# One token list per expert for both router choices, with the weighted rows added to the output by the scatter itself

## The chip, the cores and the metric

The kernel runs on one core of a Trainium2 chip. The metric is the device time of one execution in microseconds (us); the profile shows one execution of its own, with its span from the first to the last instruction.

## The reference, cut to what matters

The input is 2048 tokens (8 batches of 256) of 512 numbers. A gated cross attention is added to each token, and then a gated mixture of 8 experts, of which each token uses the two with the highest router probability:

```
x = x + tanh(g_xattn) * cross_attention(layernorm(x), ctx, mask)
h = layernorm(x)
p = softmax(h @ w_router.T)                  # 8 experts
v, i = top_k(p, 2);  v = v / sum(v)
x = x + tanh(g_ffn) * sum over the two choices k:
        v[k] * (silu(h @ w_gate[i[k]].T) * (h @ w_up[i[k]].T)) @ w_down[i[k]].T
```

An expert has 192 inner columns. All numbers are 32-bit floats.

## The kernel before

**Attention stage.** The tokens are cut into 16 tiles of 128. The order of the instructions on every engine is written by hand: a loop over steps `s` calls the parts of a tile (`a_scores`, `a_probs`, `a_values`) and of a pair of tiles (`f_scale`, `f_weigh`, `f_mark`, `f_rank`, `f_table`, `f_count`) at fixed offsets, and each engine works through its own list in that order. `a_values` (line 397) adds the attention to the residual tile in `xall`. `f_weigh` finishes a pair's rows `xr`: 512 centred columns, the router logits, the negative mean `NM`, the two choice weights `W1` and `W2` and two scales. It stores them to a table `xc_d` in memory with a DMA issued by ACT (line 427, 576 KB each, eight of them). Loads are issued by SP in the same loop: `load_batch` brings the transposed tokens of a batch, three buffers deep, and `load_half` brings one half of an expert's weights (`wgu` 768 KB or `wd` 384 KB) in each of the steps 2 to 17.

**Routing.** For each choice there is a separate list of tokens per expert, filled up to whole tiles of 128. `f_mark`, `f_rank` and `f_count` count with matmuls into `rank`; `f_table` writes the token numbers into `table` with matmuls. The factors `ac` of these (line 458) are made on POOL. At the end, `numbers`, `read_table` and `experts` turn this into `ids`, the row numbers of every list tile, and `eqi`, the expert of every tile.

**Expert stage.** `run` goes over 19 tiles of the first choice and then 19 tiles of the second. For a tile `q`, POOL issues an indirect gather of 128 rows of `xc_d` into a ring of eight buffers that lies over `xall` (line 681); it is issued four tiles ahead. PE transposes the rows (`turn`, line 183), multiplies by `wgu_sb` (`gate_up`, line 699), transposes the result (`flip`, line 714) and multiplies by `wd_sb` (`down`, line 723). The expert of the tile is a register, so the slices of `wgu_sb` and `wd_sb` are addressed at run time, and the first `gate_up` waits for the loads of all experts' `wgu`. ACT applies the choice's weight while it copies the result to `y` (line 727). A first-choice tile then adds the residual on DVE (line 729) and POOL scatters it to a second table `acc_d` (line 686). A second-choice tile gathers its rows of `acc_d`, adds them on DVE (`add`, line 736, one step after `down`) and POOL scatters the sum to `out`. The scatters are declared independent of each other (`free`), so none waits for the one before it. Unused places of a tile gather one row of zeros, and the scatter drops them. If a list needs more than 19 tiles, a branch (`more_tiles`) runs the rest one after the other; it stands once between the two lists and once at the end.

Of the kernel before, what the change touches and what calls it, by code (L numbers as in the profile page):

```python
# [28 lines left out]
NL = 2 * E  # L29
LT = T // P  # L30
NQ = NT + E - 1
Q2 = NQ
NS = 2 * NQ
CV = 64
NP = B // 2
N0 = NT + 3
E1 = E + 1
LG, NM, W1, W2, RS, R2 = D, D + E, D + E1, D + E1 + 1, D + E1 + 2, D + E1 + 3
XU = D + E1 + 4
# [7 lines left out]
def gated_xattn_moe(ctx: ExitStack, tc: tile.TileContext, x, xT, ctxn, ctxT, mask, maskT, g_x, g_f, wr, wgu, wd, out):  # L47
# [84 lines left out]
    ntg = const.tile([P, 1], FP, name="ntg")  # L132
# [12 lines left out]
    xc_d = dr.tile([T + 1, XW], FP, name="xc_d")  # L145
    acc_d = dr.tile([T + 1, D], FP, name="acc_d")
# [3 lines left out]
    table = bank([P, 2, P], "table")  # L150
# [3 lines left out]
    ecol = const.tile([P, 2, E], FP, name="ecol")  # L154
    lbase = const.tile([1, P], FP, name="lbase")
    ltile = const.tile([P, 2, E], FP, name="ltile")
    keep = const.tile([P, 2, E], FP, name="keep")
    cols = const.tile([P, P], FP, name="cols")
    idt = const.tile([P, NT], FP, name="idt")
# [6 lines left out]
    marks = [rt.tile([P, 2 * NL + P], FP, name=f"mark_{k}") for k in range(2)]  # L166
# [3 lines left out]
    spacer = const.tile([1, 1], FP, name="spacer")  # L170
# [68 lines left out]
    def m_gates():  # L239
        nc.vector.tensor_scalar(few, KEEP["most"], float(CV), None, ALU.is_le)  # L240
        nc.vector.tensor_scalar(vgt, cnt, 1.0, few, ALU.min, ALU.mult)
        nc.vector.tensor_scalar(ntg, tg[:, 1:2], -1.0, None, ALU.mult)
        nc.vector.tensor_scalar(vgt, vgt, tg[:, 0:1], None, ALU.mult)
        pairs = vgt.rearrange("p (n h) -> p h n", h=2)
        for h in range(2):
            nc.vector.tensor_copy(vcol[h * CV:(h + 1) * CV, :], pairs[h * CV:(h + 1) * CV, h, :])
        nc.vector.tensor_scalar(nvcol, vcol, -1.0, None, ALU.mult)
# [171 lines left out]
    def f_weigh(k):  # L419
# [5 lines left out]
        nc.scalar.activation(xr[:, :, W1], d, AF.Identity, bias=tg[:, 1:2], scale=ntg)  # L425
        nc.scalar.activation(xr[:, :, W2], d, AF.Identity, bias=tg[:, 1:2], scale=tg[:, 1:2])
        nc.scalar.dma_start(out=xc_d[2 * k * P:2 * (k + 1) * P, :].rearrange("(t p) c -> p t c", p=P), in_=xr)

    def f_mark(k):
        m = marks[k % 2][:, NL:3 * NL]  # L430
        nc.vector.tensor_tensor(m.rearrange("p (t k e) -> p t k e", t=2, k=2), ecol.unsqueeze(1).broadcast_to([P, 2, 2, E]),
                                ix[:, 2 * k:2 * k + 2, 0:2].unsqueeze(3).broadcast_to([P, 2, 2, E]), ALU.is_equal)

# [3 lines left out]
    def f_rank(k):  # L437
        more(k, below, NL)
        more(k, ones, 0)
        at = sm_.tile([P, 2 * NL], FP, tag="at", bufs=2, name=f"at_{k}")  # L440
        nc.vector.tensor_mul(at, marks[k % 2][:, NL:3 * NL], rank[:, 0:2 * NL])
        pos = sm_.tile([P, 4], I32, tag="pos", bufs=2, name=f"pos_{k}")
        with nc.allow_low_precision(reason="whole numbers under 2 ** 16"):
            nc.vector.tensor_reduce(pos, at.rearrange("p (n e) -> p n e", n=4), AX.X, ALU.add)
# [10 lines left out]
        for n in range(4):  # L455
            i = 2 * k + n // 2
            by = nc.vector if last and n < 2 else nc.gpsimd
            by.tensor_scalar(at_col[:, n, :], cols, low[:, n:n + 1], idt[:, i:i + 1], ALU.is_equal, ALU.mult)  # L458
        KEEP["at", k] = at_row, at_col

    def f_table(k):

        at_row, at_col = KEEP.pop(("at", k))
        for n in range(4):
            nc.tensor.matmul(table[:, n % 2, :], lhsT=at_row[:, n, :], rhs=at_col[:, n, :], start=False, stop=True,  # L465
                             skip_group_check=True)

    def f_count(k):
        more(k, rest, NL)
        more(k, ones, 2 * NL)  # L470

    def free(inst, group):

        nc.gpsimd.memset(spacer, 0.0)
        inst = inst.ins
        tc.declare_no_dep(inst, group=group, reason="other rows")
        tc.add_to_no_dep_group(group, inst)

    def constants():
# [4 lines left out]
        nc.gpsimd.iota(lbase[:, 0:2 * NL].rearrange("o (t k e) -> o t k e", t=2, k=2), pattern=[[0, 2], [0, 2], [T, E]], base=0, channel_multiplier=0,  # L484
# [7 lines left out]
    def more_constants():  # L492
        any_ = dict(allow_small_or_imprecise_dtypes=True)
        nc.gpsimd.iota(ecol, pattern=[[0, 2], [1, E]], base=0, channel_multiplier=0, **any_)
# [5 lines left out]
        nc.gpsimd.iota(idt, pattern=[[P, NT]], base=-T, channel_multiplier=1, **any_)  # L500
        for t in xrs:
            nc.gpsimd.memset(t[:, :, XU:XW], 0.0)
        nc.gpsimd.dma_start(out=xc_d[T:T + 1, :], in_=zero)
        nc.gpsimd.dma_start(out=acc_d[T:T + 1, :], in_=zero[:, 0:D])

    def last_constants():
        any_ = dict(allow_small_or_imprecise_dtypes=True)
        nc.gpsimd.iota(ltile, pattern=[[0, 2], [-LT, E]], base=0, channel_multiplier=0, **any_)
        nc.gpsimd.memset(keep, 1.0)
        nc.gpsimd.memset(keep[:, 1, 0:1], 0.0)  # L510
# [14 lines left out]

    ids = rt.tile([P, NS], U32, name="ids")
    eqi = rt.tile([1, NS], I32, name="eqi")
    nt_i = rt.tile([1, 2], I32, name="nt_i")
    sel = rt.tile([P, 2, NQ], FP, name="sel")

    end = rt.tile([P, 2, E], FP, name="end")

    def numbers():

        u = rt.tile([P, 2, E], I32, name="u")
        uf, lf = u.rearrange("p k e -> p (k e)"), ltile.rearrange("p k e -> p (k e)")
        nc.vector.tensor_scalar(uf, rank[:, 0:NL], float(P - 1), None, ALU.add)
        nc.vector.tensor_scalar(uf, uf, 7, None, ALU.arith_shift_right)
        nti = rt.tile([P, 2, E], FP, name="nti")
        nf = nti.rearrange("p k e -> p (k e)")  # L540
        nc.vector.tensor_tensor(nf, uf, lf, ALU.add)
        nc.vector.tensor_tensor_scan(end.rearrange("p k e -> p (k e)"), keep.rearrange("p k e -> p (k e)"), nf, 0.0,
                                     ALU.mult, ALU.add)
        nc.vector.tensor_sub(nti, end, nti)
        nc.vector.tensor_mul(nti, nti, rowe.unsqueeze(1).broadcast_to([P, 2, E]))
        begin = rt.tile([P, 2], FP, name="begin")
        nc.vector.tensor_reduce(begin, nti, AX.X, ALU.add)
        for k in range(2):
            nc.vector.tensor_scalar(sel[:, k, :], qplace, begin[:, k:k + 1], None, ALU.is_equal)

    def experts():
        past = row([P, NS * E], "past")[0:1].rearrange("o (k q e) -> o k q e", k=2, q=NQ)
        nc.vector.tensor_tensor(past, end[0:1].unsqueeze(2).broadcast_to([1, 2, NQ, E]),
                                cols[0:1, 0:NQ].unsqueeze(1).unsqueeze(3).broadcast_to([1, 2, NQ, E]), ALU.is_le)
        pn = rt.tile([1, NS], FP, name="pn")
        nc.vector.tensor_reduce(pn, past.rearrange("o k q e -> o (k q) e"), AX.X, ALU.add)
        nc.vector.tensor_scalar(eqi, pn, float(E - 1), None, ALU.min)
        nc.vector.tensor_copy(nt_i, end[0:1, :, E - 1])

    def read_table():  # L560
        tb = row([P, 2, P], "tb")
        nc.scalar.copy(tb, table)
        pid = bank([P, NS], "pid")
        for k in range(2):
            nc.tensor.matmul(pid[:, k * NQ:(k + 1) * NQ], lhsT=tb[:, k, :], rhs=sel[:, k, :], start=True, stop=True)
        nc.vector.tensor_scalar(ids, pid, float(T), None, ALU.add)
# [5 lines left out]
    with tc.manual_schedule(engines={PE, DVE, ACT, POOL, SP}):  # L572
# [32 lines left out]
        for s in range(NT + 2):  # L605
# [32 lines left out]
            if s == 1:  # L638
                nc.tensor.matmul(rank, lhsT=ones[0:1, :], rhs=lbase, start=True, stop=True)
                nc.tensor.matmul(table.rearrange("p k r -> p (k r)"), lhsT=ones[0:1, :], rhs=zero[:, 0:2 * P], start=True, stop=True)  # L640
# [22 lines left out]
            if part == 0 and 0 < p < NP:  # L663
                m_route(p)
            if not odd and 3 <= (s + 4) // 2 < B:
                load_batch((s + 4) // 2)
            if 2 <= s < 2 + 2 * E:
                load_half(s - 2)

# [3 lines left out]
    def gather(src, q, name):  # L673
        if name == "xg":
            k = RING if apart else KEEP["ring"]
            g = xall.rearrange("p i d -> p (i d)")[:, k * XW:(k + 1) * XW]
            if not apart:
                KEEP["ring"] = (k + 1) % RING
        else:
            g = row([P, D], f"{name}_{q}")  # L680
        nc.gpsimd.indirect_dma_start(out=g, out_offset=None, in_=src[:, :],  # L681
                                     in_offset=bass.IndirectOffsetOnAxis(ap=ids[:, q:q + 1], axis=0))
        KEEP[name, q] = g

    def scatter(dst, q, z, group):
        free(nc.gpsimd.indirect_dma_start(out=dst, out_offset=bass.IndirectOffsetOnAxis(ap=ids[:, q:q + 1], axis=0),  # L686
                                          in_=z, in_offset=None, bounds_check=T - 1, oob_is_err=False), group)
# [31 lines left out]
    def down(q):  # L719
# [6 lines left out]
        c = W1 if q < Q2 else W2  # L726
        nc.scalar.activation(y, py, AF.Copy, scale=xg[:, c:c + 1])  # L727
        if q < Q2:
            nc.vector.scalar_tensor_tensor(y, xg[:, 0:D], xg[:, NM:NM + 1], y, ALU.subtract, ALU.add)  # L729
            scatter(acc_d[:, :], q, y, "acc")  # L730
        else:
            KEEP["y", q] = y

    def add(q):
        y, a = KEEP.pop(("y", q)), KEEP.pop(("acc", q))
        nc.vector.tensor_add(y, y, a)  # L736
        scatter(out, q, y, "out")

    AHEAD, LAG = 4, 3

    def run(qs, side=None, after=None):

        n = len(qs)

        def at(f, s, *more):
            if 0 <= s < n:
                f(*more[:1], qs[s], *more[1:]) if more else f(qs[s])
        for s in range(min(AHEAD, n)):
            at(gather, s, xc_d, "xg")
        for s in range(min(2, n)):  # L750
            at(turn, s)
        for s in range(n + LAG):
# [67 lines left out]
```

## Time and profile before

| what | value |
|---|---|
| median of 3 runs | 300.09 us (299.21 to 300.32) |
| the profiled execution, its own time | 298.8 us |
| its span | 297.0 us |
| PE busy | 265.2 us, 89% of the span |
| POOL busy | 152.8 us, 51% |
| DVE, ACT busy | 133.2 us (45%), 114.6 us (39%) |
| DMA | 48.55 MB, 163 GB/s over the span |
| granted TensorE clock, mean | 0.96 |

The profiled execution took 1.8 us more than its span, and is 1.3 us under the median. In the page a line such as L699 is a line of the kernel's code; PE is TensorE, PEld its weight loads, POOL is GpSimd, SP the engine that issues most loads. "Landing" of a DMA is the moment at which its semaphore tells that all of it has arrived.

### The profile page before, as it was taken

How to read it: one execution, taken by the hardware profiler on the slowest of the kernel's cores; microseconds unless marked ns; L12 is line 12 of the kernel's file. 1: busy time of each engine (PE TensorE's matmuls, PEld its weight loads, DVE VectorE, ACT ScalarE, POOL GpSimd, SP SyncE). 2: the span in 40 equal slices, each digit the busy share in tenths (PEclk: the TensorE clock that was granted, in tenths of full speed). 3: DMA queues.
4: the chain of work that ended last, by engine and by line, in shares of the span. 5: the costliest groups of instructions: out<-in, count | busy, mean ns of one | idle time of the engine just before them, and what ended most of it. 6: DMA issues, size and time to landing. Idle time of an engine off the chain costs nothing.

```text
span 297.0 us, 4010 instructions
## 1 busy us (share of the span) xinstructions
PE 265.2 (89%) x1106; PEld 167.1 (56%) x1106; DVE 133.2 (45%) x450; ACT 114.6 (39%) x275; POOL 152.8 (51%) x239
## 2 busy tenths in 40 slices
PE   5489688979963899999999999998999999999990
PEld 4186477767742565656565656564555555555550
DVE  3438878887772033333333333333233333252441
ACT  2123567777770133333333333332322432333330
POOL 4508964647574502534343434342677578465452
PEclk9959999999995599999999999999999999999997
DMA  4599847999425702232414232422465456444422
GB/s 144 202 355 384 300 164 236 295 341 360 183 104 177 230 8 74 78 115 93 135 48 138 95 124 92 122 100 78 117 206 191 138 171 210 152 142 121 141 78 98
DMA packets 16077, 48.55 MB, mean 163 GB/s; under 512 B 3181, under 2 KB 3181, under 8 KB 16048
## 3 DMA queue, kind: packets, MB, share of 16 engines
q0 software_dynamic: 7984, 25.64, 27.5%
q1 hardware_dynamic: 5888, 17.85, 17.5%
q10 hardware_dynamic: 2176, 4.72, 4.1%
q8 instruction: 13, 0.21, 0.3%
q14 instruction: 16, 0.13, 0.1%
HBM read 35.08 MB, written 14.68 MB: 168 GB/s over the span
## 4 chain that ended last, share of the span: by engine, by line
PE 45%; POOL 15%; issue 15%; DMA 8%; ACT 6%; DVE 4%; ACTq 0%; POOLq 0%; another core or an unknown queue 0%
PE pgu L699 19%; PE py L723 10%; POOL out L686 5%; POOL acc L681 4%; POOL xall L681 4%; DMA xall<-xc_d,ids 4%; PE pt_g L183 3%; PE psc L361 3%; DMA cn<-ctxn,gid 3%; PE table L465 2%; PE pav L391 2%; PE pht L714 1%; PE pc L279 1%; PE ppt L389 1%; DMA acc<-acc_d,ids 1%
## 5 line engine op out<-in xcount | busy, mean ns | idle before, releaser
L699 PE MATMUL pgu<-wgu_sb,xT_g 128*128 x304 | 106.1, 492 | 0.9 <-ACTq L772 0.9
L699 PEld LDWEIGHTS pgu<-wgu_sb,xT_g 128*128 128x128 f32 x304 | 58.1, 192 | 49.3 <-issue 17.7
L723 PE MATMUL py<-wd_sb,hT 96*128 x152 | 71.4, 592 | 0.0
L705 DVE SCALAR_TENSOR_TENSOR th<-th,pgu 128x192 f32<-128x192 f32 x38 | 13.4, 354 | 96.6 <-ACT th L704 71.6
L686 POOL DMA_INDIRECT acc_d<-y,ids x19 | 19.3, 1018 | 60.4 <-DVE y L729 57.8
L681 POOL DMA_INDIRECT xall<-xc_d,ids x38 | 38.7, 1018 | 13.1 <-issue 6.2
L704 ACT ACTIVATE th<-pgu,xall 128x192 f32<-128x192 f32 x38 | 16.0, 420 | 72.4 <-PE pgu L699 55.9
L727 ACT ACTIVATE y<-py,xall 128x512 f32<-128x512 f32 x38 | 26.1, 688 | 37.7 <-PE py L723 29.3
L723 PEld LDWEIGHTS py<-wd_sb,hT 96*128 96x128 f32 x152 | 25.9, 190 | 18.7 <-issue 18.7
L185 ACT COPY xT_g<-pt_g 128x512 f32<-128x512 f32 x38 | 22.2, 585 | 26.3 <-PE pt_g L183 15.4
L458 POOL TENSOR_SCALAR ac<-cols,low,idt 128x128 f32<-128x128 f32 x30 | 25.4, 856 | 11.6 <-DVE low L448 11.5
L686 POOL DMA_INDIRECT out<-y,ids x19 | 20.0, 1051 | 21.6 <-DVE y L736 16.1
L183 PE MATMUL pt_g<-ident,xall 128*128 128x128 f32 x152 | 23.8, 281 | 5.5 <-issue 4.9
L729 DVE SCALAR_TENSOR_TENSOR y<-xall,y 128x512 f32<-128x512 f32 x19 | 14.3, 751 | 28.7 <-ACT y L727 27.2
L681 POOL DMA_INDIRECT acc<-acc_d,ids x19 | 18.3, 963 | 9.7 <-issue 9.7
L183 PEld LDWEIGHTS pt_g<-ident,xall 128*128 128x128 f32 x152 | 18.3, 144 | 6.6 <-issue 5.5
L361 PE MATMUL psc<-cT,xT 128*128 128x137 f32 x128 | 19.6, 301 | 1.3 <-issue 0.7
L361 PEld LDWEIGHTS psc<-cT,xT 128*128 128x128 f32 x128 | 17.9, 208 | 2.0 <-issue 1.1
L714 PEld LDWEIGHTS pht<-ident,h 128*96 128x96 f32 x76 | 9.6, 126 | 12.7 <-issue 7.6
L391 PE MATMUL pav<-cn,prT 128*128 128x512 f32 x32 | 16.4, 594 | 0.0
L707 DVE SCALAR_TENSOR_TENSOR h<-th,xall,pgu 128x192 f32<-128x192 f32 x38 | 15.7, 414 | 1.4
L716 DVE COPY hT<-pht 96x256 f32<-96x256 f32 x38 | 15.8, 415 | 0.6 <-remote 0.4
(156 smaller groups left out, 298.6 us busy)
## 6 DMA issues: line engine op xcount, KB each, us to landing
wgu_sb<-wgu SPq DMA_DIRECT2D x8, 768.0 KB, 7.2
xc_d<-xr ACTq DMA_DIRECT2D x8, 576.0 KB, 7.7
xT<-xT SPq DMA_DIRECT2D x8, 512.0 KB, 5.8
wd_sb<-wd SPq DMA_DIRECT2D x8, 384.0 KB, 7.1
xall<-x SPq DMA_DIRECT2D x1, 2048.0 KB
xall<-x SPq DMA_DIRECT2D x2, 512.0 KB
xall<-x SPq DMA_DIRECT2D x1, 1024.0 KB, 6.9
xall<-xc_d,ids POOLq DMA_INDIRECT x38
```

The costliest lines, as they stand in the source:

```text
L183: nc.tensor.transpose(pt[:, c, :], src[:, c * P:(c + 1) * P], ident)
L185: nc.scalar.copy(dst, pt)
L361: nc.tensor.matmul(both, lhsT=xTs[b][:, c, t * P:(t + 1) * P], rhs=cTs[p % 2][:, c, :], start=(c == 0), stop=(c == HC - 1))
L391: nc.tensor.matmul(pav, lhsT=prT, rhs=cns[p], start=True, stop=True)
L458: by.tensor_scalar(at_col[:, n, :], cols, low[:, n:n + 1], idt[:, i:i + 1], ALU.is_equal, ALU.mult)
L681: nc.gpsimd.indirect_dma_start(out=g, out_offset=None, in_=src[:, :], in_offset=bass.IndirectOffsetOnAxis(ap=ids[:, q:q + 1], axis=0))
L686: free(nc.gpsimd.indirect_dma_start(out=dst, out_offset=bass.IndirectOffsetOnAxis(ap=ids[:, q:q + 1], axis=0), in_=z, in_offset=None, boun ...
L699: nc.tensor.matmul(pgu, lhsT=xgT[:, c, :], rhs=wgu_sb[:, bass.ds(v * GU + c * 2 * I, 2 * I)], start=(c == 0), stop=(c == HC - 1))
L704: nc.scalar.activation(th, pgu[:, 0:I], AF.Tanh, scale=xg[:, RS:RS + 1])
L716: nc.vector.tensor_copy(hT, pht)
L723: nc.tensor.matmul(py, lhsT=hT[:, k, :], rhs=wd_sb[:, bass.ds(v * DN + k * D, D)], start=(k == 0), stop=(k == 1))
L727: nc.scalar.activation(y, py, AF.Copy, scale=xg[:, c:c + 1])
```

## The change

The two lists are merged into one list per expert, in which a token stands twice, under two experts. The list has 36 tiles (`N0 = 2 * NT + 4`), with up to 39 places in all. Which choice a place belongs to is told by the sign and size of its number in `table` (`idt` has two columns), and `read_table` makes from it `ids` and a `sign` of -1 or +1. Instead of `W1` and `W2` a row holds one number `DW`, and DVE makes each tile's weight column `w` from `DW`, `sign` and the gate.

The residual no longer goes through the expert stage. A new `x_store` writes each pair of finished residual tiles (512 KB) from `xall` to `out` through SP's queue in the attention loop. In the expert stage, every tile's weighted `y` is scattered to `out` by POOL with `compute_op=ALU.add`: the DMA adds the rows to what `out` holds. These scatters are not declared independent any more, so each waits for the landing of the one before it. `acc_d`, its gathers, both DVE additions, `free` and the middle branch are gone. Unused places now read and write 128 rows of their own behind the tokens, in `xc_d` and in `out`, which three DMAs on POOL's queue fill with zeros in `more_constants`.

The last four half loads of weights (experts 6 and 7) move from the steps 14 to 17 of the loop to behind the loop.

```diff
-        nc.scalar.activation(xr[:, :, W1], d, AF.Identity, bias=tg[:, 1:2], scale=ntg)
-        nc.scalar.activation(xr[:, :, W2], d, AF.Identity, bias=tg[:, 1:2], scale=tg[:, 1:2])
+        nc.scalar.activation(xr[:, :, DW], d, AF.Copy, scale=tg[:, 1:2])
...
     def f_mark(k):
-        m = marks[k % 2][:, NL:3 * NL]
-        nc.vector.tensor_tensor(m..., ecol..., ix..., ALU.is_equal)
+        hot = sm_.tile([P, 4, E], FP, tag="hot", bufs=2, name=f"hot_{k}")
+        nc.vector.tensor_tensor(hot..., ecol..., ix..., ALU.is_equal)
+        nc.vector.tensor_add(marks[k % 2][:, E:3 * E]..., each[:, :, 0, :], each[:, :, 1, :])
...
-        nc.gpsimd.dma_start(out=xc_d[T:T + 1, :], in_=zero)
-        nc.gpsimd.dma_start(out=acc_d[T:T + 1, :], in_=zero[:, 0:D])
+        nc.gpsimd.dma_start(out=xc_d[T:T + P, 0:D], in_=busy)
+        nc.gpsimd.dma_start(out=xc_d[T:T + P, D:XW], in_=busy[:, 0:XW - D])
+        nc.gpsimd.dma_start(out=out[T:T + P, :], in_=busy)
...
     def read_table():
-        tb = row([P, 2, P], "tb")
+        tb = row([P, P], "tb")
         nc.scalar.copy(tb, table)
-        pid = bank([P, NS], "pid")
-        for k in range(2):
-            nc.tensor.matmul(pid[:, k * NQ:(k + 1) * NQ], lhsT=tb[:, k, :], rhs=sel[:, k, :], start=True, stop=True)
-        nc.vector.tensor_scalar(ids, pid, float(T), None, ALU.add)
+        pid = bank([P, NQ], "pid")
+        nc.tensor.matmul(pid, lhsT=tb, rhs=sel, start=True, stop=True)
+        part = rt.tile([P, 2, NQ], FP, name="part")
+        nc.vector.tensor_scalar(part[:, 0, :], pid, 0.0, prow, ALU.is_equal, ALU.mult)
+        nc.vector.tensor_scalar(part[:, 1, :], pid, -float(T) - 0.5, 2.0 * T, ALU.is_lt, ALU.mult)
+        nc.vector.scalar_tensor_tensor(part[:, 0, :], pid, float(T), part[:, 0, :], ALU.add, ALU.add)
+        nc.vector.tensor_tensor(ids, part[:, 0, :], part[:, 1, :], ALU.add)
+        nc.vector.tensor_scalar(sign, part[:, 1, :], 1.0 / T, -1.0, ALU.mult, ALU.add)
+
+    def x_store(k):
+        nc.sync.dma_start(out=out[2 * k * P:2 * (k + 1) * P, :].rearrange("(i p) d -> p i d", p=P), in_=xall[:, 2 * k:2 * k + 2, :])
...
+            if not odd:
+                on(x_store, (s - 2) // 2, NT // 2)
             if not odd and 3 <= (s + 4) // 2 < B:
                 load_batch((s + 4) // 2)
-            if 2 <= s < 2 + 2 * E:
+            if 2 <= s < 2 + 2 * E - 4:
                 load_half(s - 2)
+        for n in range(2 * E - 4, 2 * E):
+            load_half(n)
...
-        c = W1 if q < Q2 else W2
-        nc.scalar.activation(y, py, AF.Copy, scale=xg[:, c:c + 1])
-        if q < Q2:
-            nc.vector.scalar_tensor_tensor(y, xg[:, 0:D], xg[:, NM:NM + 1], y, ALU.subtract, ALU.add)
-            scatter(acc_d[:, :], q, y, "acc")
-        else:
-            KEEP["y", q] = y
+        w = sm_.tile([P, 1], FP, tag="w", name=f"w_{q}")
+        nc.vector.tensor_scalar(w, xg[:, DW:DW + 1], sign[:, q:q + 1], tg[:, 1:2], ALU.mult, ALU.add)
+        nc.scalar.activation(y, py, AF.Copy, scale=w)
+        nc.gpsimd.indirect_dma_start(out=out[:, :], out_offset=bass.IndirectOffsetOnAxis(ap=ids[:, q:q + 1], axis=0),
+                                     in_=y, in_offset=None, compute_op=ALU.add)
...
+    AHEAD = 4
+    def run(n):
+        for q in range(AHEAD):
+            gather(q)
+        for q in range(2):
+            turn(q)
+        for q in range(n + 2):
+            on(gather, q + AHEAD, n)
+            on(gate_up, q, n)
+            on(flip, q - 1, n)
+            on(turn, q + 2, n)
+            on(down, q - 2, n)
...
     with tc.manual_schedule(engines={PE, DVE, ACT, POOL, SP}):
-        run([*range(N0), *range(Q2, Q2 + N0)], lambda: more_tiles(0), N0 - 1)
-        more_tiles(1)
+        run(N0)
+        more_tiles()
```

## The prediction

> **What bounds the kernel now.** I read the page first, then busy time by stage (`PEclk` is the granted TensorE clock), then the list of waits, and last the engines' timelines where two stages meet.
>
> ```profile
> 83.00:99.50 16.50, 8.53 (x41) 6.27 (x41) 6.78 (x31) 6.02 (x18) 9.97 (x12) 0.69 0.48 162
> 110.00:195.00 85.00, 85.00 (x314) 49.48 (x313) 31.50 (x69) 29.19 (x52) 33.97 (x51) 1.00 0.31 98
> 212.00:286.00 74.00, 74.00 (x264) 42.22 (x263) 25.69 (x61) 23.59 (x43) 47.11 (x60) 1.00 0.51 158
> 286.00:297.00 11.00, 4.15 (x12) 1.58 (x10) 3.25 (x6) 2.06 (x3) 4.27 (x8) 0.86 0.28 105
> ```
>
> The first pair of numbers after the stretch's length is PE. In the two long stretches of the expert stage PE is busy every microsecond at full clock; DVE, ACT, POOL and the DMA engines all have room. So the stage is worth a fixed PE time per tile: the first `pgu` matmuls of successive tiles start at 112.41, 117.36, 122.32 ... 196.66, a pitch of 4.956 us. Only three places are not PE-bound: the passage from attention to experts (83 to 99.5), the passage between the lists (195 to 212), and the end.
>
> ```profile
> L699 PE MATMUL pgu<-wgu_sb,xT_g 128*128 x304 | 106.1, 492 | 0.9 <-ACTq L772 0.9
> L686 POOL DMA_INDIRECT acc_d<-y,ids x19 | 19.3, 1018 | 60.4 <-DVE y L729 57.8
> L729 DVE SCALAR_TENSOR_TENSOR y<-xall,y 128x512 f32<-128x512 f32 x19 | 14.3, 751 | 28.7 <-ACT y L727 27.2
> L681 POOL DMA_INDIRECT acc<-acc_d,ids x19 | 18.3, 963 | 9.7 <-issue 9.7
> ```
>
> The reader sees that the removed work (POOL's `acc` gathers, DVE's additions, here L729 and likewise L736) runs on engines that wait for PE's chain. Removing it gains nothing by itself; the removed tiles gain.
>
> **Part 1: two tiles fewer, and no middle branch.** 38 tiles become 36. I worked out the reference's routing: the merged lists hold 510, 475, 538, 516, 620, 527, 494 and 416 tokens, so 4+4+5+5+5+5+4+4 = 36 tiles, and the last branch stays empty. Gain 2 x 4.956 = 9.9 us. Around the middle branch one pitch is 202.63 - 196.66 = 5.97 and one 5.18 (212.64 to 217.82): 1.01 + 0.22 = 1.2 us more. Sum -11.1 us. `w` (36 DVE operations, about 0.15 us each by the smallest one-column rows) stands behind `hT` on DVE and before the `py` matmuls end; DVE's 63% of idle time covers it, else it would cost 0.15 us a tile.
>
> **Part 2: the scatter chain.** Each scatter waits on POOL for the previous one's landing. Behind the waiting scatter of tile q stands the gather of tile q+7, whose rows PE turns two iterations later. At 115.70 such a gather is issued, it lands 3.7 us later by the trace's landing record, and its turn comes at about 125: some 5.6 us of slack. So the chain costs nothing in the steady stage as long as one link (landing plus wake-up) stays under 4.956 us. What is a link?
>
> ```profile
> 291.75:292.00 0.25, 0.00 (x0) 0.00 (x0) 0.00 (x0) 0.00 (x0) 0.12 (x1) 1.00 0.00 0
> ...
> 293.00:293.25 0.25, 0.00 (x0) 0.00 (x0) 0.00 (x0) 0.00 (x0) 0.00 (x0) 1.00 0.12 33
> 293.25:293.50 0.25, 0.00 (x0) 0.00 (x0) 0.00 (x0) 0.00 (x0) 0.00 (x0) 1.00 0.37 147
> 293.50:293.75 0.25, 0.00 (x0) 0.00 (x0) 0.00 (x0) 0.00 (x0) 0.00 (x0) 1.00 0.93 360
> 293.75:294.00 0.25, 0.00 (x0) 0.00 (x0) 0.00 (x0) 0.00 (x0) 0.00 (x0) 0.88 0.77 295
> ```
>
> This is the last plain scatter: issued at 291.88, its packets flow from 293.0 to 294.0, and the trace's landing record is 294.4, so 2.6 us in all. An `out` row is now also read. The nearest rows for a read of 128 rows from memory are the gathers: 3.1 us for `acc` (283.86 to 286.95), 3.4 to 3.7 us for `xc_d`. Lower bound: the added read overlaps fully, 2.6 us. Upper bound: gather and scatter one after the other, 3.5 + 2.6 = 6.1 us. I take 4.1 us: the scatter's 2.6, the gather's 0.5 longer way, and a second microsecond of packets because twice the bytes pass. Wake-up of POOL is 0.3 us (DVE's addition ends at 260.63, its scatter starts at 260.90). Link: 4.4 us, hidden by 0.5 us.
>
> The Trainium skill, "DMA: Bandwidth & Descriptors", section "Anatomy of one DMA — SWDGE (gpsimd) path", gives a fixed 2.0 us plus bytes over 436 GB/s; for the doubled bytes, 2.0 + 0.524/0.436 = 3.2 us, a link of 3.5. It treats reading as free of latency, while the gathers here take 0.5 to 1.1 us more than the scatter, so I stay with 4.1. The same page, section "Rules for kernel authors", says that nothing holds a row between an accumulating DMA's read and its write, so that a second writer must wait for the first's semaphore: a token's two rows can stand in neighbouring tiles, and the wait cannot be dropped. No run here has shown an accumulating DMA yet.
>
> At the end the chain is not hidden. ACT's last three `y` end at 287.22, 289.16 and 290.88 (in before's times), only 1.8 us apart.
>
> ```profile
> 288.38 1.00 POOL L686 DMA_INDIRECT out<-y,ids  x1 [0.24 <-issue]
> 290.48 0.98 POOL L686 DMA_INDIRECT out<-y,ids  x1 [1.03 <-DVE y L736]
> 291.88 0.98 POOL L686 DMA_INDIRECT out<-y,ids  x1 [0.34 <-issue]
> ```
>
> Before, they left as they came. Now they leave at 287.5, 291.9 and 296.3, and the last lands at 300.4 instead of 294.4: +6.0 us (the DVE addition that is gone is in this). By the skill's figure: 287.5 + 3.5 + 3.5 + 3.2 = 297.7, +3.3 us.
>
> **Part 3: the passage to the experts.** `x_store` of the last pair waits for line 397 of tile 15, which ends at 85.1. Behind it in SP's queue now stand the four half loads that before were issued by 70.7: 0.52 + 2.36 = 2.9 MB released at 85.2, just when the last two `xc_d` stores (1.18 MB, ACT at 87.72 and 89.41) go out. Before, they had the DMA engines to themselves:
>
> ```profile
> 86.00:88.00 2.00, 0.85 (x5) 0.66 (x6) 1.78 (x9) 1.70 (x7) 1.15 (x2) 1.00 0.00 0
> 88.00:90.00 2.00, 1.46 (x7) 0.98 (x7) 1.67 (x10) 1.18 (x5) 1.62 (x3) 0.78 0.67 270
> 90.00:92.00 2.00, 1.52 (x6) 1.11 (x5) 0.00 (x0) 0.37 (x1) 0.00 (x0) 0.50 0.85 320
> 92.00:94.00 2.00, 0.00 (x0) 0.00 (x0) 1.42 (x5) 0.00 (x0) 0.85 (x1) 0.50 0.00 0
> ```
>
> ```profile
> DMA to landing us min/median/max: 2.9/7.7/11.0
> ```
>
> The second is the `xc_d` stores' landing: 2.9 us alone, up to 11.0 in the saturated attention stage. The last two columns of the first are DMA share and GB/s: the stores are through at 92, and the first gather, which needs all of them and `ids` (92.22), starts at 93.15. Now 4.06 MB pass from 86.2 on; at 360 GB/s (busy slices show 300 to 384) that is 11.3 us, until 97.5. If the stores come last, the first gather is 5.3 us late; if the two queues share evenly they are through by about 95, 3 us late. I take +4.0. The first `gate_up` also waits for all `wgu`, by 97.5, before its 103.5: no further cost. In `read_table`, four DVE operations of 0.2 us replace one and a matmul pair (0.5 us) goes; the extra 0.3 us lies under the stores' landing and would cost 0.3 us without it.
>
> **Part 4: the attention stage.** POOL's two zero-filling DMAs (0.64 + 0.53 us) become three, of 128 rows in place of one:
>
> ```profile
> 30.19 0.64 POOL L503 DMA_DIRECT2D xc_d<-zero  x1
> 30.83 0.53 POOL L504 DMA_DIRECT2D acc_d<-zero  x1
> ...
> 34.78 3.14 POOL L458 TENSOR_SCALAR ac<-cols,low,idt 128x128 f32<-128x128 f32 x4
> ```
>
> Priced like the indirect ones of 128 rows, 1.0 us each, POOL is 1.9 us later (at least 0.6). Behind them stand the fetches of `cn`, and `ac`, which `table`'s matmuls already await at 37.1 to 38.3; PE's list stands behind those, so nearly all shows: +1.5 us. Against it, SP issues the loads of 20.80 to 22.1 (1.7 MB) only after `x_store(0)` at 29, so the `cn` fetch that lands at 30.19 may land sooner; DVE waits 0.97 us for it. DVE gains one small operation a pair (8 x 0.19 us), ACT loses one (8 x 0.38); I set these three against each other at nothing, +1/-1 us. The eight `x_store` issues cost SP 0.4 us each, and SP is idle. But each `load_batch` is now behind an `x_store`: the last at 63.6 instead of 56.5, needed at 74.8; landing takes 5.8 us in the median, so it is hidden by 5 us, with up to 12.6 us seen it would stall PE 1.4 us.
>
> **Sum**, on the profiled 298.8 us: -11.1 + 6.0 + 4.0 + 1.5 = +0.4. Carried to the median, 300.09 + 0.4 = 300.5 us.
>
> **The rivals.** (1) The chain sets the pitch. Mechanism: an accumulating scatter's landing, from 4.66 us up; place: POOL's wait in every tile. The first `y` ends at 113.3 + 5.5, so the first scatter goes at 119.1; with a link of 5.2 us the last lands at 119.1 + 35 x 5.2 + 4.9 = 306.0, 11.6 us later than now: 311.7 us. With 5.6: 326. At the upper bound, 6.4: 355. For it: no row shows the added read; against: 0.5 us of room over an estimate from gathers. (2) The added read is nearly free: link 2.9, the end costs 287.5 + 5.8 + 2.6 - 294.4 = +1.5, the sum is -4.1, 296.0 us; with the evenly shared queues 295. For it: DMA share is 0.31 to 0.51 in these stages. (3) The released loads choke the `xc_d` stores as in the saturated stage (11.0 us): the gather starts at 101.3, +8, sum +4.4: 304.5. (4) The change doesn't do what it says: a 37th tile would run through the branch; the nearest expert is 2 tokens from its limit, so 1 in 100.
>
> **How the numbers follow.** The sum with hidden chain (rival 3 being its upper end): 53%, with an own range of 297.5 to 304.5. The chain as pitch: 29%. The free read: 18%. Under 0.5%, 1.5 us, a measurement of this kernel can't tell a difference. Of the 53%, 7 fall below, 27 within and 19 above this bound. Faster 0.07 + 0.18 = 0.25; same 0.27; slower 0.19 + 0.29 = 0.48. The slower ones are spread over three mechanisms, so the likeliest single account remains 300.5. The range: 296 leaves out some 7%, 316 leaves out links above 5.3 us, some 12%.
>
> **What would show it.** Right: first scatter about 5 us later than 114.36; `pgu` pitch 4.956; three scatters at the end 4.4 us apart, POOL waiting for DMA `out`; first gather near 97. Wrong: a `pgu` pitch over 5 us with `pt_g` or `y` waiting on POOL or a DMA (rival 1); a first gather by 94; scatters at the end under 3 us apart; PE waiting for `xT` in attention.

## The result, and the profile after

The changed kernel takes 329.83 us (median of 4 runs, 328.93 to 330.58) against 300.2 us before (4 runs, 299.21 to 301.36) in the same place: a ratio of 1.098, with a 95% interval of 1.094 to 1.103. The forecast was 300.5 us with a range of 296 to 316; the time lies outside it. The profiled execution took 328.93 us (before 298.8), its span is 327.2 us (before 297.0).

Busy time by stage first (length; PE, PEld, DVE, ACT, POOL busy; PE clock, DMA share, GB/s), for the same places as before:

```profile
83.00:99.50 16.50, 5.77 (x30) 4.03 (x30) 7.56 (x37) 4.66 (x15) 5.45 (x7) 0.78 0.85 282
110.00:159.00 49.00, 49.00 (x184) 28.86 (x183) 13.39 (x41) 16.58 (x30) 18.00 (x14) 1.00 0.41 80
159.00:195.00 36.00, 32.32 (x113) 17.68 (x112) 7.68 (x24) 10.86 (x19) 15.57 (x13) 1.00 0.54 99
212.00:286.00 74.00, 67.39 (x236) 36.97 (x235) 16.63 (x52) 22.03 (x39) 33.51 (x26) 1.00 0.54 100
286.00:327.20 41.20, 16.86 (x53) 8.42 (x51) 4.62 (x15) 5.29 (x9) 10.91 (x7) 0.76 0.36 50
```

Until 159 us PE is busy every microsecond, as before. From there on it is not, though the granted clock stays at 1.00. Of the last 41 us PE is busy for 16.9, none of it after 303, where before the end took 11 us. The starts of `pgu` tell the same: from 114.60 up to 159.21 they are 4.956 us apart, then come 164.65, 170.18, 176.30, 181.48, 187.66, 193.93. PE is no longer the bound. The waits (engine and line, what it waited for, total us, times, longest) name what is:

```profile
POOL out L722 <- DMA out<-y,ids: 68.7, 24, 4.1
PE pt_g L177 <- DMA xall<-xc_d,ids: 26.0, 22, 13.8
PEld pt_g L177 <- DMA xall<-xc_d,ids: 17.6, 23, 1.3
```

POOL waits up to 4.1 us in front of a scatter (L722) for the landing of the one before; PE waits for gathers that stand behind those scatters in POOL's list (its longest wait, 13.8, is the passage to the experts). The groups of the page agree: the scatter is now its costliest line.

```profile
L722 POOL DMA_INDIRECT out<-y,ids x36 | 57.0, 1584 | 118.1 <-DMA out<-y,ids 68.7
L692 PE MATMUL pgu<-wgu_sb,xT_g 128*128 x288 | 99.8, 489 | 0.0
L678 POOL DMA_INDIRECT xall<-xc_d,ids x36 | 35.5, 986 | 22.0 <-DMA xc_d<-xr 11.3
```

The second number after the first bar shows that an accumulating scatter holds POOL for 1.58 us, where the plain one took 1.02. POOL's timeline of the end (start, duration, idle before it) shows the chain alone, since the last gather is issued at 283.43:

```profile
298.41 1.55 POOL L722 DMA_INDIRECT out<-y,ids  x1 [4.21 <-ACT th L697]
304.01 1.55 POOL L722 DMA_INDIRECT out<-y,ids  x1 [4.05 <-ACTq L743]
309.60 1.55 POOL L722 DMA_INDIRECT out<-y,ids  x1 [4.05 <-DMA out<-y,ids]
315.30 1.55 POOL L722 DMA_INDIRECT out<-y,ids  x1 [4.15 <-issue]
320.96 1.55 POOL L722 DMA_INDIRECT out<-y,ids  x1 [4.11 <-DMA out<-y,ids]
```

The starts are 5.6 to 5.7 us apart. (The releaser named in brackets is not always the DMA; the distance from start to start decides.) The last `y` was ready at 299.98; the five scatters drain a backlog until 325.70. For one link the trace has both ends: issued at 315.30, landed at 320.14, next scatter at 320.96. That is 4.84 us of landing and 0.82 us until POOL goes on, 5.66 in all, against PE's 4.956. The first fence below has the landings of all `out` transfers; the second has POOL's first gather at the passage to the experts, before and after:

```profile
DMA to landing us min/median/max: 3.3/4.8/6.0
```

```profile
93.15 1.12 POOL L681 DMA_INDIRECT xall<-xc_d,ids  x1 [3.52 <-DVE past L553]
101.19 1.11 POOL L678 DMA_INDIRECT xall<-xc_d,ids  x1 [11.34 <-DMA xc_d<-xr]
```

The first gather starts 8.0 us later than before, and POOL sat idle for 11.3 us until the last table store had landed. So there are two losses at two places. The experiments separate them.

### The profile page after: what moved, and what is told of

Same layout as the page of the kernel before. It is cut to its first block, busy times and chain, and to the rows that moved or that the text cites. A ratio compares the mean times of both kernels' runs of the same rounds, so it can differ in the third digit from the quotient of the medians.

```text
span 327.2 us, 3773 instructions
## 1 busy us (share of the span) xinstructions
PE 258.5 (79%) x1068; PEld 159.5 (49%) x1068; DVE 113.2 (35%) x452; ACT 109.0 (33%) x261; POOL 147.6 (45%) x178
## 5 line engine op out<-in xcount | busy, mean ns | idle before, releaser
L722 POOL DMA_INDIRECT out<-y,ids x36 | 57.0, 1584 | 118.1 <-DMA out<-y,ids 68.7
L692 PE MATMUL pgu<-wgu_sb,xT_g 128*128 x288 | 99.8, 489 | 0.0
L692 PEld LDWEIGHTS pgu<-wgu_sb,xT_g 128*128 128x128 f32 x288 | 54.9, 192 | 45.1 <-issue 16.7
L716 PE MATMUL py<-wd_sb,hT 96*128 x144 | 67.6, 592 | 0.0
L678 POOL DMA_INDIRECT xall<-xc_d,ids x36 | 35.5, 986 | 22.0 <-DMA xc_d<-xr 11.3
L721 ACT ACTIVATE y<-py,w 128x512 f32<-128x512 f32 x36 | 24.7, 687 | 40.1 <-PE py L716 40.1
L177 PEld LDWEIGHTS pt_g<-ident,xall 128*128 128x128 f32 x144 | 16.2, 145 | 32.7 <-DMA xall<-xc_d,ids 17.6
L707 PE MATMUL pht<-ident,h 128*96 128x128 f32 x72 | 13.7, 273 | 0.0
L463 PE MATMUL table<-ac,ar 128*128 128x128 f32 x64 | 10.8, 291 | 2.9 <-POOL ac L456 1.5
L463 PEld LDWEIGHTS table<-ac,ar 128*128 128x128 f32 x64 | 8.9, 190 | 8.3 <-POOL ac L456 5.1
```

The source lines that it names most:

```text
L177: nc.tensor.transpose(pt[:, c, :], src[:, c * P:(c + 1) * P], ident)
L463: nc.tensor.matmul(table, lhsT=at_row[:, n, :], rhs=at_col[:, n, :], start=False, stop=True, skip_group_check=True)
L678: nc.gpsimd.indirect_dma_start(out=g, out_offset=None, in_=xc_d[:, :], in_offset=bass.IndirectOffsetOnAxis(ap=ids[:, q:q + 1], axis=0))
L692: nc.tensor.matmul(pgu, lhsT=xgT[:, c, :], rhs=wgu_sb[:, bass.ds(v * GU + c * 2 * I, 2 * I)], start=(c == 0), stop=(c == HC - 1))
L707: nc.tensor.transpose(pht[:, k, :], h[:, k * IH:(k + 1) * IH], ident)
L716: nc.tensor.matmul(py, lhsT=hT[:, k, :], rhs=wd_sb[:, bass.ds(v * DN + k * D, D)], start=(k == 0), stop=(k == 1))
```

## The experiments

**Theory.** The serial wait of each accumulating scatter on the one before it sets the pitch of the expert stage (link 5.66 us), and the 8 us at the passage are a separate loss, made by DMA volume that the change puts in front of the last table stores. Rivals: the accumulating DMA loads POOL or the memory so that everything slows; the fewer, larger lists are slower on PE; the two losses hide in each other, so that mending one gives nothing.

### e1_plain: the wait stays, the addition goes

```diff
-                                     in_=y, in_offset=None, compute_op=ALU.add)
+                                     in_=y, in_offset=None)
```

The rows are written, not added, so the sum of the residual and a token's two rows is left out. Row numbers and unused places are still those of the changed kernel.

> The scatters of the changed kernel write their rows plainly (no compute_op), each still waiting for the landing of the one before; so the addition to the residual and of a token's two rows is left out. Theory (the accumulating scatter's landing, 4.84 us, plus 0.82 us of wake-up make a link of 5.66 us and set the pitch): a plain link is 2.6 + 0.3 = 2.9 us, the pgu pitch returns to 4.956, the time to about 299 us (start +7.9, tiles -11.1, end +1.5 against before). Rival (the pitch is set by late gathers and the loads that now overlap the experts, whatever the scatter does): 320 us or more. If it is the wait's wake-up that is long and not the addition, the last three scatters stand 3.5 us or more apart.

Measured 297.69 us, ratio to before 0.995 (0.992 to 0.998). The waits and the landings of this kernel:

```profile
POOL out L722 <- ACT y L721: 102.1, 33, 12.5
POOL out L722 <- DMA out<-y,ids: 5.6, 2, 3.1
```

```profile
DMA to landing us min/median/max: 2.7/2.7/8.1
```

In 33 of 36 cases the scatter waits for its own `y`, and `pgu` keeps 4.956 us to the end. At the end of this kernel one plain link is 292.22 - 288.74 = 3.48 us: 2.70 us to landing and 0.78 until the next. I had expected 2.9; the difference is nearly all in the 0.78. So in the steady stage the wait for the previous landing is by itself free; what makes it dear is the 2.1 us that the addition puts on the landing.

### e2_two_deep: the addition stays, half of the wait goes

```diff
+    spacer = const.tile([1, 1], FP, name="spacer")
...
-        nc.gpsimd.indirect_dma_start(... compute_op=ALU.add)
+        if q < N0:
+            nc.gpsimd.memset(spacer, 0.0)
+        inst = nc.gpsimd.indirect_dma_start(... compute_op=ALU.add).ins
+        KEEP["out", q] = inst
+        if 2 <= q < N0:
+            tc.declare_no_dep(inst, KEEP["out", q - 1], reason="other rows")
```

Each scatter waits for the last but one. This is allowed because, with these tokens, no two neighbouring tiles hold the same token. The one-element `spacer` is written between two scatters (0.09 us in the median).

> The accumulating scatters wait for the one two before instead of the one before (neighbouring tiles share no row with these data). Theory (the wait in series is what costs, not the addition's own traffic): pitch 4.956 us, last three scatters overlap in pairs, about 300 us (start +7.9, tiles -11.1, end +3.5). Rival (two additions in flight fill the DMA engines, since one keeps them at a share of 0.9 for 2.5 to 3.3 us, and a gather of 1.5 us comes on top): pitch 5.2 to 5.7, 310 to 328 us.

Measured 296.88 us, ratio 0.994 (0.992 to 0.996).

```profile
POOL out L725 <- ACT y L722: 68.5, 30, 10.8
POOL out L725 <- DMA out<-y,ids: 14.2, 5, 3.5
```

```profile
DMA to landing us min/median/max: 3.3/4.9/8.3
```

```profile
159.00:195.00 36.00, 36.00 (x131) 20.76 (x130) 8.95 (x28) 12.55 (x22) 18.64 (x21) 1.00 0.63 117
212.00:286.00 74.00, 74.00 (x261) 41.68 (x259) 19.97 (x63) 24.62 (x44) 35.89 (x43) 1.00 0.58 98
```

The landings are as long as in the change (4.9 us), POOL is as loaded and the DMA engines are more so (share 0.58 instead of 0.54), yet PE is busy throughout again. That rules out a general slow-down, and it rules out that the merged lists are slower on PE: only the serial wait was too long. It came out some 3 us under the 300 that I expected. The end is not the reason: the last landing comes 7.3 us after the last `y` (294.23 and 286.92) where it was 3.7 before, so the end costs 3.6, as expected (3.5). About 1 us is the place, where the kernel before takes 299.25; 0.9 is the time from the last landing to the end of the span (1.5 us instead of 2.4); 0.6 is the start, since the third `pgu` comes 7.3 us later than before and not 7.9.

### e4_loads_early: the chain stays, the passage is undone

```diff
-    def x_store(k):
+    def x_store(k, by=nc.sync):
...
-                on(x_store, (s - 2) // 2, NT // 2)
+                on(x_store, (s - 2) // 2, 5)
...
-            if 2 <= s < 2 + 2 * E - 4:
+            if 2 <= s < 2 + 2 * E:
                 load_half(s - 2)
-        for n in range(2 * E - 4, 2 * E):
-            load_half(n)
...
+            if q < 3:
+                x_store(5 + q, nc.scalar)
```

> The chain is untouched; the weights of experts 6 and 7 are loaded in the steps 14 to 17 again, and the last three residual stores are issued by ACT beside the first three expert tiles, so nothing large is released beside the last two stores of rows. Theory (2.9 MB of released loads delay those stores and so the first gather by 8 us, and with it the whole chain): first gather near 94 instead of 101.2, and all of it shows at the end, 322 to 323 us. Rival (the chain absorbs a later start, or the saturated attention stage only gets longer): 327 us or more.

Measured 323.1 us, ratio 1.082 (1.075 to 1.090).

```profile
93.78 1.11 POOL L676 DMA_INDIRECT xall<-xc_d,ids  x1 [3.57 <-DVE nt_i L545]
```

```profile
POOL out L720 <- DMA out<-y,ids: 60.6, 21, 4.1
```

The first gather is back at 93.78. The bracket names DVE's `nt_i`, but the gather needs only `ids`, done at 92.29, and the table stores. The last of these lands at 92.89, 3.4 us after its issue (11.2 in the change), and the gather starts 0.89 us later, as it does in the change (100.30 to 101.19). The whole kernel is 6.7 us shorter than the change (6.5 by the spans, 320.7 and 327.2), while POOL's wait for the landings stays. The two losses do not hide in each other.

### e3_loads_only: which DMAs delay the table stores?

```diff
-            if 2 <= s < 2 + 2 * E - 4:
+            if 2 <= s < 2 + 2 * E:
                 load_half(s - 2)
-        for n in range(2 * E - 4, 2 * E):
-            load_half(n)
```

> One part of the change undone: the four half loads of experts 6 and 7 stand in the steps 14 to 17 of the loop again. The eight stores of residual pairs stay on SP's queue where the change put them; the chain of accumulating scatters is untouched. The run before this one that moved the loads back also moved the last three residual stores to another place, and gained 6.7 us. Theory A, the released loads alone made the last table stores late: first gather at 93.8 to 95, some 6.5 us earlier than the changed kernel's 101.2, and a time of about 323 us. Theory B, the residual stores beside the table stores were the cause: the last 512 KB store still goes out at 85.4 just ahead of the table stores, so the first gather stays at 97 or later and the time is 326 us or more. Theory C, the loads push the attention stage itself back when they share it with the residual stores: the residual of tile 15 is finished later than 84.6, by a few us, and the gain is lost there: 326 to 330 us.

Measured 326.56 us, ratio 1.087 (1.083 to 1.090). By its numbers (97 or later, 326 us or more) this is theory B, though only just, and the gather still comes 3.6 us earlier than in the change: the loads have a part in it. POOL's first gather, SP's last issues, and the DMA share:

```profile
97.58 1.11 POOL L676 DMA_INDIRECT xall<-xc_d,ids  x1 [7.61 <-DMA xc_d<-xr]
```

```profile
79.53 0.47 SPq L137 DMA_DIRECT2D wgu_sb<-wgu  x1
80.05 1.00 SPq L139 DMA_DIRECT2D wd_sb<-wd  x1
85.51 0.40 SPq L561 DMA_DIRECT2D out<-xall  x1
85.95 0.47 SPq L137 DMA_DIRECT2D wgu_sb<-wgu  x1
86.46 0.82 SPq L139 DMA_DIRECT2D wd_sb<-wd  x1
```

```profile
84.00:86.00 2.00, 1.92 (x14) 1.43 (x12) 1.51 (x8) 1.34 (x4) 1.45 (x3) 1.00 0.95 291
86.00:88.00 2.00, 0.84 (x6) 0.52 (x4) 1.65 (x8) 1.66 (x7) 1.15 (x2) 1.00 1.05 394
88.00:90.00 2.00, 1.49 (x6) 1.05 (x6) 1.76 (x10) 0.81 (x4) 1.97 (x3) 0.81 1.10 351
```

Theory C fails: tile 15's residual starts at 84.7, as in the change (84.62).

The edit puts the loads back in the loop, but it moves only half of them away from the table stores. In SP's list each residual store waits for its tile, and the loads stand behind it: expert 6's leave at 79.53 and 80.05, expert 7's at 85.95 and 86.46, behind the last residual store (85.51) and just ahead of the table stores (87.7 and 89.3). In the kernel before all four had left by 70.7. Of the 8.0 us, 3.6 go with this edit (101.19 to 97.58). Another 3.8 go in e4_loads_early (97.58 to 93.78), which takes the last three residual stores off SP's queue and by that also lets the last loads leave by 79.53; what these stores cost by themselves is not shown. What goes with the delay in all the runs is the volume. From 86 us until the table stores have landed 1.2 MB pass before, 2.0 in e4_loads_early, 3.4 here and 4.06 in the change, and the last landing is at 92.3, 92.89, 96.78 and 100.30.

### g_half_rows: what is in the link?

```diff
-        nc.gpsimd.indirect_dma_start(... ap=ids[:, q:q + 1] ...
-                                     in_=y, in_offset=None, compute_op=ALU.add)
+        nc.gpsimd.indirect_dma_start(... ap=ids[0:64, q:q + 1] ...
+                                     in_=y[0:64, :], in_offset=None, compute_op=ALU.add)
```

> What is in a link of 5.66 us? Each accumulating scatter passes on only the first 64 of a tile's 128 rows (the other half of the addition is left out); the wait of each scatter for the one before it, the gathers and everything else are as in the changed kernel. Theory A, the link is mostly fixed (a read and then a write of memory, one after the other, and POOL's wake-up), and rows count little: issue about 1.4 us, landing about 4.4, link 5.2, last landing at 121 + 35 x 5.2 + 4.4 = 307.4, a time near 310 us. Theory B, rows and bytes make what the addition costs over the plain scatter (landing 4.84 against 2.7 us): issue about 1.0, landing about 3.7, link 4.5, under PE's pitch of 4.956 us: the pgu pitch falls back to 4.956 and the time is near 299 to 301 us.

Measured 298.92 us, ratio 0.997 (0.993 to 1.001): the verdict of theory B. The scatters of this kernel (ns min/median/max), and the landings of all `out` transfers:

```profile
L722 POOL DMA_INDIRECT out<-y,ids x36: 1395/1432/1510, 120.3 to 291.5; - x36
```

```profile
DMA to landing us min/median/max: 3.3/3.7/5.4
```

Half of the addition is left out here. The last two landings are 3.54 and 3.63 us, so 64 rows less save 1.2 us, and the link is 291.51 - 287.22 = 4.29 us, under 4.956. Theory B's detail on the issue was wrong: half the rows still take 1.43 us on POOL, so that most of the longer issue comes with the addition and not with the rows.

### f_both: two-deep chain and undone passage together

The edits of e2_two_deep and e4_loads_early in one kernel.

> Both edits together: the chain two deep and the loads early. If the two causes are separate and add up: 300 - 7.5 = 292 to 293 us, under the kernel before (300.1). If the two-deep chain still sets the pitch: 303 us or more. If the early loads only move the wait: 299 to 300 us.

Measured 291.08 us (289.4 to 292.53), ratio to before 0.973 (0.966 to 0.979): faster than both kernels.

```profile
POOL out L723 <- ACT y L720: 69.7, 30, 12.5
```

```profile
94.47 1.11 POOL L677 DMA_INDIRECT xall<-xc_d,ids  x1 [3.43 <-DVE past L541]
```

The gains of the two edits add up: the ratios of the separate runs give 1.098 - 0.104 - 0.016 = 0.978, within the interval of this one. The version is only as good as its condition that neighbouring tiles share no token; this holds for this routing and not for any. A version for any routing would have to keep the wait where a tile's expert differs from the one before; it was not tried.

## Why the prediction was wrong, point by point

**Part 2, the chain: the step that failed.** The sum took the link as 4.4 us, "hidden by 0.5 us"; it is 5.66 us and not hidden. The rule behind it held: links of 3.48 us (e1_plain) and 4.29 us (g_half_rows) cost nothing in the steady stage, and one of 5.66, over the pitch of 4.956, sets the pace. What failed is the size of two terms.

The landing, taken as 4.1 us, is 4.84. It was inside the bounds of 2.6 to 6.1; the estimate was 2.6 for the plain scatter, 0.5 for the longer way and 1.0 for a second microsecond of packets. The packet records of the traces divide both landings. A plain one (2.7 us in e1_plain) is 1.5 us to the first packet, 0.8 us of packets and 0.35 to the landing record; the accumulating one is 2.1, 2.4 and 0.3. So the packets cost 1.6 us more and not 1.0, which is most of the error. The first packet comes 0.6 us later, as much as POOL is held longer (1.55 against 0.97 us); the sum had 0.5 there, for another reason. The stretches from 315.30 on show the packets (last columns DMA share and GB/s). Their shares make 1.96 us per engine, against 0.55 in the stretches of the plain scatter that the prediction shows:

```profile
316.30:317.30 1.00, 0.00 (x0) 0.00 (x0) 0.00 (x0) 0.00 (x0) 0.55 (x1) 0.50 0.00 0
317.30:318.30 1.00, 0.00 (x0) 0.00 (x0) 0.00 (x0) 0.00 (x0) 0.00 (x0) 0.50 1.07 115
318.30:319.30 1.00, 0.00 (x0) 0.00 (x0) 0.00 (x0) 0.00 (x0) 0.00 (x0) 0.50 0.83 137
319.30:320.30 1.00, 0.00 (x0) 0.00 (x0) 0.00 (x0) 0.00 (x0) 0.00 (x0) 0.50 0.06 10
```

The bytes do not double in these records: both kinds show 262 KB, the plain one in 64 packets and the accumulating one in 128. Whether the read or the addition makes the packets slow is not shown; with half the rows they take 1.3 us.

The wake-up, taken as 0.3 us, is 0.82 (0.78 in e1_plain, 0.75 in g_half_rows). The 0.3 was read from a scatter that waited for DVE, not for a DMA: the wrong row. With the second error alone the chain would still have been hidden (4.1 + 0.82 = 4.92), with the first alone it would have been 0.2 us a tile over the pitch (4.84 + 0.3 = 5.14). Together they make 0.7 us a tile. The estimate from the Trainium skill ("DMA: Bandwidth & Descriptors", "Anatomy of one DMA — SWDGE (gpsimd) path"), 3.2 us of landing for the doubled bytes, lay further off; here the measurement decides. (The page's list of what the fixed part consists of names no read; it does not say that a read costs nothing.)

**Rival 1 is what happened.** Its mechanism, its place and its formula held (for a link of 5.6 it gave 326 us): 119.1 + 35 x 5.66 + 4.84 = 322.0 for the last landing, and 2 us more because the first scatter came at 121.05; the trace has 325.70, with a mean link of 5.71. The slack of the gathers showed too, though it was smaller than the 5.6 us of the prediction: the first gather behind a scatter is issued at 123.02, its rows are turned at 132.27, and with a landing of 4.2 us that leaves 5.0. At 0.75 us a tile this lasts 6 to 7 tiles. The gather of tile 13, behind the scatter of tile 6, is the first that comes too late (turned at 162.44 instead of 162.0), and the pitch of `pgu` stays at 4.956 until tile 11 (159.21; the first tile is 0), while POOL was already running late.

**Part 3, the passage: mis-sized.** "+4.0" is +8.0, the price of rival 3, and at its place: it had the first gather at 101.3. The volume was right: the two-microsecond stretches from 86 to 100 sum to 2 x (290 + 230 + 249 + 291 + 395 + 399 + 178) = 4064 KB, the 4.06 MB of the sum. Two things were not. The queues did not share evenly: the table stores, issued at 87.59 and 89.15, landed at 99.02 and 100.30, with the last of the volume, and for that the prediction itself had 5.3 us. The other 2.7 are the rate: it was taken as 360 GB/s, and the first four of these stretches show 230 to 291. Why it is lower there stays open.

**Part 1 held.** Two tiles fewer and no middle branch: the pitch is 4.956 in every run in which the chain is hidden (e1_plain, e2_two_deep, g_half_rows, f_both), and the last branch stayed empty. From the third `pgu` to the last it is 174.36 us before (107.45 to 281.81) and 163.11 in e1_plain (114.63 to 277.74), 11.25 less against the 11.1 of the sum. **Part 4 was too dear.** The three zero-filling DMAs take 0.68, 0.57 and 0.55 us, not 1.0 each; `ac` starts at 35.60 instead of 34.78, and tile 15's residual at 84.62 instead of 84.36: +0.3 us in place of +1.5.

```profile
31.06 0.57 POOL L495 DMA_DIRECT2D xc_d<-busy  x1
31.60 0.55 POOL L496 DMA_DIRECT2D out<-busy  x1
...
35.60 3.15 POOL L456 TENSOR_SCALAR ac<-cols,low,idt 128x128 f32<-128x128 f32 x4
```

The ledger against the profiled 298.8 us: -11.1 for Part 1, +7.9 for the first `pgu` (107.42 against 99.49, with Part 4 in it), and what is left of the measured +30.1, that is +33.3, for Part 2, where the forecast had +6.0. The runs with the chain taken apart (32.1 us less in e1_plain, 32.9 in e2_two_deep) agree with that within 1.2 us, or within 2.1 if the 1 us is taken off by which the kernel before is faster beside them.

## What to carry to other kernels

A chain of dependent transfers costs nothing while one link is shorter than the pitch of the bound engine and costs its whole excess in every tile beyond that, so an estimate of the link that comes as near to the pitch as here (4.4 to 4.956) decides nothing; take the wake-up from a row where the engine waits for a DMA. If the data allow it, splitting the chain into two interleaved ones takes it out as well as a shorter link does (296.9 us here, against 297.7 with a plain link and 298.9 with half the rows), and it leaves no work out. A large store moved into a stage with free DMA share is not free when a small store at the stage's end releases the next one: count the bytes in front of that store on all queues together. And a store that waits for its data holds back every load behind it in its queue.

## What the runs showed of the hardware that I had not expected

- An accumulating scatter of 128 rows of 2 KB holds POOL for 1.55 to 1.66 us and lands after 4.85 us in the median of the 36 in e4_loads_early (4.6 to 5.8); a plain one takes 0.97 to 1.02 and 2.7. With 64 rows the accumulating one still holds POOL for 1.43 us and lands after 3.6.
- The same 262 KB are 64 packets in 0.8 us when they are written plainly (e1_plain) and 128 packets in 2.4 us when they are added.
- From the landing of a scatter to the next on POOL that waits for it, 0.75 to 0.97 us pass (0.80 in the median of the 35 links of e4_loads_early), with and without the addition; the first gather starts 0.80 to 0.89 us after the last table store has landed, in three kernels.
- Table stores on ACT's queue, alone 2.9 us to landing, took 11.4 and 11.2 us beside 2.9 MB on SP's queue, whose last load landed at 98.83: they came in with the last of it, not with an even share.
